# Mamba scan: the input delta·u·B and the convolution moved to TensorE

## The chip, the cores and the metric

The kernel runs on one core of a Trainium2 chip. The metric is the device time of one execution in microseconds (us). Three runs of the kernel before gave 3393.25, 3393.28 and 3399.04 us, so its time is 3393.28 us, the median. A profile is one more execution, recorded instruction by instruction; its own span counts from the first to the last instruction.

Engines: PE is TensorE (PEld its loading of weights), DVE is VectorE, ACT is ScalarE, POOL is GpSimd, SP is the engine that only issues DMAs here. Each works its own queue in order.

## The reference, cut to what matters

Two layers run one after the other; the change is in the first one, a Mamba block beside a feed-forward network with fp4-quantized weights and activations. There are 8 batches of 512 tokens, 256 features, 512 inner channels and 16 states.

```python
xz = jnp.einsum('bld,ed->ble', x, W_in)
x_in, z = (xz[..., :d_inner], xz[..., d_inner:])
xc = lax.conv_general_dilated(x_in.transpose(0, 2, 1), conv_w, (1,), [(k - 1, 0)], feature_group_count=d_inner)
u = jax.nn.silu(xc + conv_b[None, :, None]).transpose(0, 2, 1)
x_dbl = jnp.einsum('bld,ed->ble', u, W_xproj)          # delta_raw, B_ssm, C_ssm
delta = jax.nn.softplus(jnp.einsum('blr,dr->bld', delta_raw, W_dt) + b_dt)
A = -jnp.exp(A_log)

def step(h, inp):
    d_t, u_t, B_t, C_t = inp
    dA = jnp.exp(d_t[:, :, None] * A[None])
    h = dA * h + (d_t * u_t)[:, :, None] * B_t[:, None, :]
    y_t = jnp.einsum('bdn,bn->bd', h, C_t)
    return (h, y_t)
...
y = (ys.transpose(1, 0, 2) + D_param * u) * jax.nn.silu(z)
return jnp.einsum('bld,ed->ble', y, W_out)
```

Before this the input is normalized, and its output and that of the feed-forward network are added to it.

## The kernel before

**Layout.** Channels lie on the 128 partitions (four chunks of channels, NC = 4) and time runs along the free dimension, so that one VectorE instruction scans 512 tokens of one state for 128 channels. A step g of the main loop handles two states of one chunk of one batch: 8 batches x 4 chunks x 8 pairs of states = 256 steps (STEPS = 32 a batch).

**A step.** `decay` (ACT) makes exp(delta·A) for two states into `da`. `spread_b` (PE) copies a row of B over all partitions: a bf16 matmul of a selector `sel` with `bp`, three bf16 pieces of B that together carry fp32 precision, into a PSUM tile `bu`. `product` (DVE) multiplies `bu` in place by delta·u (`du`). `scan` (DVE) runs the recurrence from `da` and `bu` into `hh`. `times_c` (POOL) multiplies `hh` by C, which a DMA on SP's queue has spread over the partitions (`cb`, fetched two steps ahead). `sum_states` (PE) turns `hh` and adds up the 16 states in the PSUM tile `y`.

**The order.** All engines keep the program order that is written out here (the class `Ordered`). At step g the loop issues: the C fetch of g+2, the sums of g-2 (or g-3), the decays of g+1, the first scan of g, the spreads of g+1, one piece of every active strand, the product with C of g-1, the second scan of g, and the products of g+1. A strand is a generator; between two of its `yield`s lie the instructions of one step. A `yield` gives how many PSUM banks of the pool `pmm` (MM = 4) the next piece needs and keeps, and the strand waits for a later step if they aren't free. Where the next chunk isn't in `ready`, the loop runs strands alone, without scans (line 769).

**The strands.** `head(b+1)` loads and normalizes x (`xn`, `xt`), projects it (`ps_in`), convolves with four taps (one on ACT, three on DVE over `cv`), makes `u`, the projection `ps_xp`, the pieces of B, and from `ps_dt` the softplus delta and `du` for two chunks at a time. It is started five steps before batch b begins. `ffn(b)` quantizes and multiplies; `output(b)` projects the gated result with `w_o`; `z` and `finish` make the gate and close a chunk; `fp4_weights` and `rotary_tables` prepare weights during batches 0 and 1.

**PSUM.** Eight banks: four for strands, three for `bu` (one state each), one for `y`.

Line numbers of the scan stage's instructions in the profile are all L50, the helper that keeps the order; the tiles' names tell them apart. The second layer (lines 800 to 1369) isn't edited.

Of the kernel before, what the change touches and what calls it, by code (L numbers as in the profile page):

```python
# [17 lines left out]
P = 128  # L18
# [18 lines left out]
RD, RC, PIECES = 32, 48, (0, 64, 96)  # L37
# [18 lines left out]
def tile_kernel(ctx: ExitStack, tc: tile.TileContext, a: dict, out: bass.AP):  # L56
# [57 lines left out]
    with ExitStack() as s0:  # L114
# [6 lines left out]
        MM = 4  # L121
        pmm = s0.enter_context(tc.tile_pool(name="pmm0", bufs=MM, space=PSUM))
        pbu = s0.enter_context(tc.tile_pool(name="pbu0", bufs=3, space=PSUM))
# [5 lines left out]
        def load_x(b):  # L129
            t = w1.tile([P, NT, D], FP, tag="x", bufs=3, name=f"x_{b}")  # L130
            sp.dma_start(t, a["x"][b].rearrange("(t p) d -> p t d", p=P))
            return t

        x_first = load_x(0)
        w_in = load(w0, chunks(a["w_in"]), [P, KC, 2 * DI], "w_in")
# [3 lines left out]
        w_xp = load(w0, chunks(a["w_xp"]), [P, NC, P], "w_xp")  # L139
# [5 lines left out]
        w_o = load(w0, chunks(a["w_o"]), [P, NC, D], "w_o")  # L145


        sel = w0.tile([P, NS, P], BF, name="sel")
        every = w0.tile([P, NS], BF, name="every")

        def constants():
            act.activation(a_neg, a_neg, AF.Exp)
            dve.tensor_scalar(a_neg, a_neg, -1.0, None, ALU.mult)
            dve.tensor_copy(every, ident[:, :NS])
            for at in PIECES[1:]:
                dve.tensor_tensor(every, every, ident[:, at : at + NS], ALU.add)
            for n in range(NS):
                dve.tensor_copy(sel[:, n, :], every[:, n : n + 1].to_broadcast([P, P]))
# [169 lines left out]
        def rotary_tables():  # L328

            for l in range(DEPTH):  # L330
                tab = rot.tile([P, 2, L], FP, tag="e", bufs=2, name="tab")
                tab = tab.rearrange("p i (t d) -> p (i t) d", d=LD).rearrange("p (i t) d -> p i t d", t=NT)
                sp.dma_start(tab, a["rotary"])
                qss = []
                for name in ("q_scale", "k_scale"):
                    qss.append(sm.tile([P, LD], FP, tag="qs", bufs=2, name="qs"))
                    sp.dma_start(qss[-1], a[name][l].unsqueeze(0).to_broadcast([P, LD]))
                yield 0, 0
                yield 0, 0
                dve.tensor_scalar(qss[0], qss[0], 8.0, None, ALU.mult)  # L340
                hd = LD // 2
                lo, hi = slice(0, hd), slice(hd, LD)
                for i, qs in ((0, qss[0]), (2, qss[1])):
                    for at, cols, sc in ((i, lo, lo), (i, hi, hi), (i + 1, lo, hi), (i + 1, hi, lo)):
                        by = qs[:, sc].unsqueeze(1).to_broadcast([P, NT, hd])
                        dve.tensor_tensor(tab[:, at, :, cols], tab[:, at, :, cols], by, ALU.mult)
                        if cols is hi:
                            yield 0, 0
                sp.dma_start(tab_d[l], tab)
                yield 0, 0  # L350

        made, xs, u_, z_, ready, through = {}, {}, {}, {}, set(), set()

        def head(b):

            x = xs[b] = load_x(b) if b else x_first
# [12 lines left out]
            dve.reciprocal(rs, rs)  # L369
            xn = w1.tile([P, NT, D], FP, tag="xn", name="xn")  # L370
# [8 lines left out]
            xt = w1.tile([P, KC, L], FP, tag="xt", name="xt")  # L379
# [8 lines left out]
            def put(k, ps):  # L388
                act.copy(xt[:, k, :], ps)
# [7 lines left out]
            def project(c, _):  # L397
                ps = pmm.tile([P, L], FP, tag="mm", name="ps_in")
                for k in range(KC):
                    pe.matmul(  # L400
                        ps, w_in[:, k, c * P : (c + 1) * P], xt[:, k, :], start=(k == 0), stop=(k == KC - 1)
# [8 lines left out]
            def tap0(c, ps):  # L410
                cv = rot.tile([P, L], FP, tag="cv", bufs=2, name="cv")
# [20 lines left out]
            stages = [(project, 0, 1), tap0, taps12, (tap3, 1, 0), silu]  # L432
            for i, need in enumerate(skewed(range(NC), stages, 2)):
                while i + 1 == len(stages) and b - 2 in u_:
                    yield 0, 0
                yield need
            u = u_[b]
            yield 1, 1
            ps = pmm.tile([P, L], FP, tag="mm", name="ps_xp")
            for c in range(NC):  # L440
                pe.matmul(ps, w_xp[:, c, :], u[:, c, :], start=(c == 0), stop=(c == NC - 1))
            yield 0, -1
            xd = w1.tile([P, L], FP, tag="xd", bufs=1, name="xd")
            act.copy(xd, ps)
            c_d = dram.tile([NS, L], FP, tag="c_d", name="c_d")
            sp.dma_start(c_d, xd[RC : RC + NS, :])

            bp = w1.tile([P, L], BF, tag="bp", name="bp")
            act.copy(bp, ps)
            yield 0, 0  # L450

            def pieces():
                for at in PIECES[1:]:
                    pool.tensor_tensor(xd[at:, :], xd[at:, :], bp[at:, :], ALU.subtract)
                    yield 0, 0
                    act.copy(bp[at:, :], xd[at:, :])
                    yield 0, 0

            delta = w1.tile([P, NC, L], FP, tag="delta", name="delta")
            du = w1.tile([P, NC, L], FP, tag="du", name="du")
            made[b] = xn, xt, bp, c_d, delta, du
# [6 lines left out]
            def parts(c, ps):  # L470
                act.activation(delta[:, c, :], ps, AF.Relu, bias=b_dt[:, c : c + 1])
                act.activation(ps, ps, AF.Abs, bias=b_dt[:, c : c + 1])
                act.activation(ps, ps, AF.Exp, scale=-1.0)
                act.activation(du[:, c, :], ps, AF.Copy, bias=1.0)
                return ps

            def rests(c, e, ps):
                w = du[:, c, :]
                dve.scalar_tensor_tensor(e[:, c % 2, :], w, 1.0, ps, ALU.subtract, ALU.subtract)

            def second(c0, ps):
                return ps, rank(c0 + 1)

            def third(c0, st):
                e = rot.tile([P, 2, L], FP, tag="e", bufs=2, name="e")
                rests(c0, e, st[0])
                return e, parts(c0 + 1, st[1])

            def fifth(c0, st):
                rests(c0 + 1, *st)  # L490
                return st[0]

            def logs(c0, e):
                w = du[:, c0 : c0 + 2, :]
                act.activation(w, w, AF.Ln)
                return e

            def sums(i):
                def f(c0, e):
                    w = du[:, c0 + i, :]  # L500
                    by.tensor_tensor(w, w, e[:, i, :], ALU.subtract)
                    return e
                return f

            def deltas(i):
                def f(c0, e):
                    c = c0 + i
                    by.tensor_tensor(delta[:, c, :], delta[:, c, :], du[:, c, :], ALU.add)
                    by.tensor_tensor(du[:, c, :], delta[:, c, :], u[:, c, :], ALU.mult)
                    ready.add((b, c))  # L510
                    return e
                return f

            by = pool if b else dve
            rest = pieces()
            stages = [
                (lambda c0, _: rank(c0), 0, 1), parts, (second, 0, 1), (third, 1, 0), lambda _, st: st, (fifth, 1, 0),
                logs, sums(0), sums(1), deltas(0), deltas(1),
# [958 lines left out]
```

## Time and profile before

| what | value |
|---|---|
| median of three runs | 3393.28 us |
| span of the profiled execution | 3396.9 us |
| first scan starts | 45.4 us |
| last scan starts | 1374.5 us |
| second layer's first PE instructions | about 1405 us |
| busy over the span: PE, DVE, ACT, POOL | 88%, 71%, 52%, 47% |
| POOL product with C (`hh`<-`hh`,`cb`), 256 of them | 604.4 us, 2363 ns each |
| ACT decay (`da`), 512 of them | 355.2 us, 718 ns each |
| ACT table loads, 242 of them | 310.5 us, 1283 ns each |
| `y` turns on PE, 2048 of them | 300.9 us busy |

How to read it: a share of busy time over the whole span mixes two stages. The scan stage is the first 1390 us or so. In the groups of the profile a line reads: source line, engine, operation, output tile <- input tiles, shapes, number, then busy us and mean ns of one, then idle time of the engine before them and who ended it. A busy PE is not a PE at its peak: matmuls overlap, and their ends are modelled. PEclk is the clock that TensorE was granted, as a share of full speed. fp32 matmuls appear as two instructions, turns (`is_transpose`) as one.

### The profile page before, as it was taken

To read this page: it belongs to the slowest core of one execution; us is meant where nothing else is said; L and a number is where in the kernel's file an instruction comes from. 1 tells how busy PE (TensorE), PEld (TensorE's weight loads), DVE (VectorE), ACT (ScalarE), POOL (GpSimd) and SP (SyncE) were. 2 spreads that over 40 slices of the span, in tenths; PEclk is the share of its full clock that TensorE was granted. 3 is DMA by queue.
4 is the path that set the end of the run, shared out by engine and by line. 5 is a ranking of instruction groups with operands and counts; after the bars stand their busy time and mean duration, and the time that the engine had idled before them with its cause. 6 is when DMAs were issued, how large, how long until landed. Compare 5 with 4: busy or idle time off the path is not lost.

```text
span 3396.9 us, 43346 instructions
## 1 busy us (share of the span) xinstructions
PE 2974.0 (88%) x15235; PEld 1723.3 (51%) x15236; DVE 2422.4 (71%) x4792; ACT 1771.3 (52%) x3500; POOL 1581.5 (47%) x1141
## 2 busy tenths in 40 slices
PE   5667787877777877899999999999999999999998
PEld 2434454545454555555554555555545545545545
DVE  7979898999999999665566466466556557556544
ACT  5666777676767776244254245244334334433533
POOL 3876777787868687333133133123223223312412
PEclk7768898989898889899999999999999999999999
DMA  3322233323232333301111101111110100100100
GB/s 107 120 90 104 97 109 102 125 93 125 96 125 96 119 105 137 108 32 52 40 38 52 45 32 52 46 49 38 42 58 32 64 33 32 64 33 32 58 33 7
DMA packets 88865, 239.55 MB, mean 71 GB/s; under 512 B 9656, under 2 KB 42424, under 8 KB 88648
## 3 DMA queue, kind: packets, MB, share of 16 engines
q1 hardware_dynamic: 87496, 232.59, 19.9%
q10 hardware_dynamic: 1152, 4.19, 0.3%
q8 instruction: 121, 1.98, 0.2%
q14 instruction: 96, 0.79, 0.1%
HBM read 227.05 MB, written 9.70 MB: 70 GB/s over the span
## 4 chain that ended last, share of the span: by engine, by line
PE 59%; DVE 26%; ACT 6%; issue 4%; POOL 4%; DMA 1%; DVEq 0%; SPq 0%; POOLq 0%; ACTq 0%
PE ps_qkv L1131 10%; DVE hh L50 10%; PE ps_g L1310 5%; PE ps_a L1310 4%; PE ps_wo L1274 3%; PE lo L1244 3%; DVE bu L50 3%; PE ps_y L1345 3%; PE ps_w L1328 3%; PE pt L1230 2%; PE y L50 2%; PE ps_ls L1183 2%; PE ps_gu L50 2%; PE ps_d L50 2%; DVE nm L997 2%
## 5 line engine op out<-in xcount | busy, mean ns | idle before, releaser
L50 POOL TENSOR_TENSOR hh<-hh,cb 128x1024 f32<-128x1024 f32 x256 | 604.4, 2363 | 177.5 <-DVE hh L50 109.4
L50 DVE TENSOR_TENSOR_SCAN hh<-da,bu 128x512 f32<-128x512 f32 x512 | 613.7, 1207 | 0.2 <-ACT da L50 0.2
L50 ACT ACTIVATE da<-delta,a_neg 128x512 f32<-128x512 f32 x512 | 355.2, 718 | 290.1 <-DVE hh L50 285.8
L50 PE MATMUL bu<-bp,sel 128*128 128x512 bf16 x511 | 197.3, 423 | 231.3 <-DVE hh L50 230.2
L50 PE MATMUL y<-ident,hh 128*128 128x128 f32 x2048 | 300.9, 298 | 89.9 <-POOL hh L50 89.7
L50 PEld LDWEIGHTS y<-ident,hh 128*128 128x128 f32 x2048 | 264.7, 155 | 179.7 <-POOL hh L50 131.8
L50 DVE TENSOR_TENSOR bu<-du,bu 128x512 f32<-128x512 f32 x512 | 324.9, 681 | 37.1 <-PE bu L50 36.8
L50 ACT ACT_TABLE_LOAD x242 | 310.5, 1283 | 23.9 <-DVE x L50 11.1
L1221 POOL TENSOR_TENSOR pr<-pr,lrs 128x512 f32<-128x512 f32 (+1 forms) x256 | 234.6, 933 | 176.6 <-DVE lrs L1219 137.7
L1150 POOL TENSOR_TENSOR r<-r,r 128x512 f32<-128x512 f32 x128 | 162.8, 1272 | 286.5 <-DVE r L1148 240.8
L1202 ACT ACTIVATE pr<-ps_ls,nm 128x256 f32<-128x256 f32 (+1 forms) x512 | 221.6, 448 | 122.4 <-DVE nm L1196 119.3
L1146 DVE TENSOR_TENSOR r<-ps_qkv,tab 128x512 f32<-128x512 f32 x128 | 88.2, 689 | 199.3 <-ACT sq L1145 195.4
L1316 ACT ACTIVATE gl<-ps_g,b 128x512 f32<-128x512 f32 x96 | 65.9, 687 | 304.1 <-PE ps_g L1310 304.1
L1048 ACT ACTIVATE pt_e<-ps_st 128x512 f32<-128x512 f32 x320 | 166.7, 596 | 107.0 <-PE ps_st L1042 100.8
L886 POOL MEMSET sa<- 128x1 f32 x16 | 1.6, 98 | 450.2 <-DVE sf L1332 356.9
L1091 POOL TENSOR_TENSOR x1s<-x1s,bsum 128x256 f32<-128x256 f32 x32 | 23.2, 724 | 370.3 <-DVE x1s L1090 370.3
L1196 DVE CUSTOM_DVE_ANT_0 ps_ls<-ps_ls,mask 128x256 f32<-128x256 f32 (+1 forms) x512 | 184.3, 422 | 5.7 <-PE ps_ls L1183 4.7
L1310 PE MATMUL ps_g<-hn,wf 128*128 128x512 f32 x384 | 183.0, 599 | 4.0 <-DVE hn L1299 2.6
L1131 PE MATMUL ps_qkv<-wqkv,sf 128*128 128x512 f32 x384 | 182.4, 608 | 0.0
L1131 PE MATMUL ps_qkv<-wqkv,s 128*128 128x512 f32 x384 | 179.8, 604 | 0.2 <-DVE r L1148 0.2
L1317 DVE SCALAR_TENSOR_TENSOR ht<-ps_a,b,gl 128x512 f32<-128x512 f32 x80 | 60.0, 750 | 157.5 <-PE ps_a L1310 157.5
L1230 PE MATMUL pt<-ident,pr 128*128 128x128 f32 x896 | 130.9, 281 | 33.0 <-POOL pr L1221 28.3
(216 smaller groups left out, 6314.5 us busy)
## 6 DMA issues: line engine op xcount, KB each, us to landing
cb<-c_d SPq DMA_DIRECT2D x256, 512.0 KB, 3.6
wqkv<-in_wqkv SPq DMA_DIRECT2D x16, 1536.0 KB, 6.8
wf<-in_wf SPq DMA_DIRECT2D x16, 1408.0 KB, 11.2
wf<-in_wf SPq DMA_DIRECT2D x16, 768.0 KB, 4.7
tab<-tab SPq DMA_DIRECT2D x18, 512.0 KB, 3.6
wo<-in_wo SPq DMA_DIRECT2D x16, 512.0 KB, 3.9
x<-in_x SPq DMA_DIRECT2D x8, 512.0 KB, 5.0
x<-x ACTq DMA_DIRECT2D x8, 512.0 KB
```

Source lines behind the costliest of these rows:

```text
L50: return self.tc.keep_in_program_order(getattr(self.engine, name)(*args, **kwargs))
L1048: act.activation(pt, banks[g], AF.Exp)
L1131: pe.matmul(ps, shifted(s, k, t * P, P), wqkv[:, k, i * IN : (i + 1) * IN], start=(k == 0), stop=(k == KC - 1),)
L1150: pool.tensor_tensor(r1[:, i], r1[:, i], r2, ALU.add)
L1196: last = dve.tensor_tensor_reduce(at, at, msk[:, 2 * P - nk :], -1.0, 3e38, ALU.add, ALU.min, nm[:, i : i + 1])
L1202: act.activation(pr[:, at], banks[r][:, at], AF.Exp, bias=nm[:, i : i + 1], scale=-1.0, accum_out=rs[:, i : i + 1],)
L1221: pool.tensor_tensor(ph, ph, rs.unsqueeze(2).to_broadcast([P, 2, nk]), ALU.mult)
L1230: pe.transpose(pt[:, j * P : (j + 1) * P], pr[:, j * P : (j + 1) * P], ident)
L1244: pe.matmul(o[r * LD : (r + 1) * LD, i * P : (i + 1) * P], lv[:, keys[j], h * LD : (h + 1) * LD], prts[r][:, (i * nkt + j) * P : (i * nkt ...
L1274: pe.matmul(ps, wo[:, c, m * P : (m + 1) * P], ot[:, c, :], start=(c == 0), stop=(c == IN // P - 1),)
L1310: pe.matmul(dst, wf1[:, k, off : off + P], hn[:, k, :], start=(k == 0), stop=(k == KC - 1))
L1328: pe.matmul(ps, wf2[:n, c, m * P : (m + 1) * P], ht[c][:n], start=(c == 0), stop=(c == NHC - 1),)
```

## The change

The spreads and products are replaced. For each chunk, delta·u is turned on TensorE (`halves_turned`, eight matmuls with the identity, one for each 64 tokens) and copied back by ACT, so that 64 tokens of the first half of time lie on partitions 0 to 63 and 64 tokens of the second half on 64 to 127. For each batch VectorE makes eight tiles `bd`, one for each pair of states: diagonals of B, 64 x 64 for each block of tokens, the two states interleaved. `inputs` then multiplies, eight fp32 matmuls of 64 rows by 128 columns a step, the two halves of time into two different PSUM banks; `scan` reads every second word. The pieces of B in bf16, `sel` and `every` go.

From batch 1 on the convolution is eight fp32 matmuls a chunk on TensorE (two halves of the features times four taps, from `xt` with four leading zeros and weights `w_c`, scaled by the taps on POOL), with bias and silu in one ACT instruction. Batch 0 keeps its taps.

To make room, PSUM's strand banks fall from four to three and `bu` has two tiles of two banks; `delta` and `du` become five buffers of one chunk each, shared by batches (HELD); the softplus runs chunk by chunk; x is loaded a second time, late, for the sums; `w_o` is loaded for every batch; `head(b+1)` starts 16 steps before batch b begins; several strands wait for buffers of others.

```diff
-RD, RC, PIECES = 32, 48, (0, 64, 96)
+RD, RC, XR = 32, 48, 64
+HELD = 5
+XP = 4
+HL = P // 2
...
-        MM = 4
+        MM = 3
         pmm = s0.enter_context(tc.tile_pool(name="pmm0", bufs=MM, space=PSUM))
-        pbu = s0.enter_context(tc.tile_pool(name="pbu0", bufs=3, space=PSUM))
+        pbu = s0.enter_context(tc.tile_pool(name="pbu0", bufs=2, space=PSUM))
...
-            dve.tensor_copy(every, ident[:, :NS])
-            for at in PIECES[1:]:
-                dve.tensor_tensor(every, every, ident[:, at : at + NS], ALU.add)
-            for n in range(NS):
-                dve.tensor_copy(sel[:, n, :], every[:, n : n + 1].to_broadcast([P, P]))
+            dve.tensor_tensor(twice, ident[:, :HL], ident[:, HL:], ALU.add)
+            for k in range(KC):
+                for i in range(4):
+                    pool.tensor_tensor(w_c[:, k, i, :], w_x[:, k, :], taps[i // 2][:, i % 2, :], ALU.mult)
...
+        def halves_turned(ps, x, n):
+
+            for t in range(NT):
+                for r in range(2):
+                    pe.matmul(
+                        ps[r * HL : (r + 1) * HL, t * n : (t + 1) * n],
+                        x[:, (r * NT + t) * HL : (r * NT + t + 1) * HL], ident[:n, :n], start=True, stop=True,
+                    )
...
-            stages = [(project, 0, 1), tap0, taps12, (tap3, 1, 0), silu]
-            for i, need in enumerate(skewed(range(NC), stages, 2)):
-                while i + 1 == len(stages) and b - 2 in u_:
-                    yield 0, 0
-                yield need
+            def convolve(k):
+                def f(c, ps):
+                    if k == 0:
+                        ps = pmm.tile([P, L], FP, tag="mm", name="ps_in")
+                    for i in range(4):
+                        pe.matmul(
+                            ps, w_c[:, k, i, c * P : (c + 1) * P], xt[:, k, XP - 3 + i : XP - 3 + i + L],
+                            start=(k == i == 0), stop=(k == KC - 1 and i == 3),
+                        )
+                    return ps
+                return f
+
+            def biased(c, ps):
+                if c == 0:
+                    u_[b] = w1.tile([P, NC, L], FP, tag="u", name="u")
+                act.activation(u_[b][:, c, :], ps, AF.Silu, bias=conv_b[:, c : c + 1])
+
+            while b - 2 in u_:
+                yield 0, 0
+            if b:
+                yield from skewed(range(NC), [(convolve(0), 0, 1), convolve(1), (biased, 1, 0)], 2)
+            else:
+                yield from skewed(range(NC), [(project, 0, 1), tap0, taps12, (tap3, 1, 0), silu], 2)
...
+            def diagonals():
+                yield 1, 1
+                ps = pmm.tile([P, L], FP, tag="mm", name="ps_bt")
+                halves_turned(ps, xd[:NS, :], NS)
+                yield 0, -1
+                bt = sm.tile([P, NT, NS], FP, tag="bt", bufs=2, name="bt")
+                act.copy(bt, ps[:, : NT * NS].rearrange("p (t n) -> p t n", n=NS))
+                yield 0, 0
+                for i in range(NS // 2):
+                    while b and clock[0] < b * STEPS - NS // 2 + i:
+                        yield 0, 0
+                    bd = rot.tile([P, NT, HL, 2], FP, tag="bd", bufs=NS // 2 + 1, name="bd")
+                    dve.tensor_tensor(
+                        bd, twice.unsqueeze(1).unsqueeze(3).to_broadcast([P, NT, HL, 2]),
+                        bt[:, :, 2 * i : 2 * i + 2].unsqueeze(2).to_broadcast([P, NT, HL, 2]), ALU.mult,
+                    )
+                    diags.append(bd)
                     yield 0, 0
...
+            def turned(c, _):
+                ps = pmm.tile([P, L], FP, tag="mm", name="ps_du")
+                halves_turned(ps, du[b, c], P)
+                return ps
+
+            def put_du(c, ps):
+                act.copy(du[b, c], ps)
+                ready.add((b, c))
...
             stages = [
-                (lambda c0, _: rank(c0), 0, 1), parts, (second, 0, 1), (third, 1, 0), lambda _, st: st, (fifth, 1, 0),
-                logs, sums(0), sums(1), deltas(0), deltas(1),
+                (lambda c, _: rank(c), 0, 1), parts, (rests, 1, 0), logs, sums, deltas, (turned, 0, 1), (put_du, 1, 0),
             ]
-            for need in skewed(range(0, NC, 2), stages, 2 if b else len(stages) - 4):
-                next(rest, None)
-                yield need
+            for c in range(NC):
+                k = b * NC + c - HELD
+                while b and (b - 1, NC - 1) not in ready or k >= 0 and divmod(k, NC) not in gated:
+                    yield 0, 0
+                active[skewed([c], stages, 1)] = 0, 0
+                for _ in range(3):
+                    yield 0, 0
...
-        def spread_b(g, i):
+        def inputs(g):
+
             b, c, n = at(g)
-            bu = pbu.tile([P, L], FP, tag="bu", name="bu")
-            pe.matmul(bu, sel[:, n + i, :], made[b][2], start=True, stop=True)
-            spreads.setdefault(g, []).append(bu)
-
-        def product(g):
-            b, c, n = at(g)
-
-
-            for bu in spreads[g]:
-                dve.tensor_tensor(bu, made[b][5][:, c, :], bu, ALU.mult)
-            hs[g] = rot.tile([P, 2, L], FP, tag="h", bufs=4, name="hh")
+            bu = spreads[g] = pbu.tile([P, 2, NT, 2 * HL], FP, tag="bu", name="bu")
+            for t in range(NT):
+                for r in range(2):
+                    rows = slice(r * HL, (r + 1) * HL)
+                    pe.matmul(
+                        bu[:, r, t, :], du[b, c][rows, t * P : (t + 1) * P],
+                        diags_[b][n // 2][rows, t, :, :].rearrange("p n i -> p (n i)"), start=True, stop=True,
+                    )
 
         def scan(g, i):
-            dve.tensor_tensor_scan(hs[g][:, i, :], decays[g][i], spreads[g][i], 0.0, ALU.mult, ALU.add)
+            if i == 0:
+                hs[g] = rot.tile([P, 2, L], FP, tag="h", bufs=4, name="hh")
+
+            bu = spreads[g].rearrange("p r t n -> p (r t n)")[:, i::2]
+            dve.tensor_tensor_scan(hs[g][:, i, :], decays[g][i], bu, 0.0, ALU.mult, ALU.add)
...
-                start(g - 5 if b else 0, (head, b + 1))
+                start(g - 16 if b else 0, (head, b + 1))
...
-            while g + 2 < total and at(g + 2)[:2] not in ready:
+            while g + 2 < total and not able(g + 2):
                 step()
```

Not shown: the loads of `taps`, `w_x` and `w_z` in place of `w_in`; the second load of x in `ffn` and the load of `w_o` in `output`; the rotary tables made in two halves; `able(g)`, which asks that the chunk is in `ready` and that the diagonal of the pair exists.

## The prediction

> **What bounds the kernel now.** I first read the slices of the page, to see which stage the edit touches.
>
> ```profile
> PE   5667787877777877899999999999999999999998
> DVE  7979898999999999665566466466556557556544
> POOL 3876777787868687333133133123223223312412
> PEclk7768898989898889899999999999999999999999
> ```
>
> The scan stage is the first sixteen slices of 85 us. There VectorE is at nine tenths, TensorE at seven to eight at a granted clock of 0.8 to 0.9. After it TensorE is full at full clock, and nothing is edited. Then I cut the stage by batch. The copies of a batch's last sum (delta<-y) start at 595.2, 759.2 and 923.1 us, so a steady batch takes 163.9 us; the busy times between them:
>
> ```profile
> 174.60:243.40 68.80, 39.29 (x139) 24.16 (x140) 44.27 (x65) 43.24 (x63) 53.97 (x37) 0.64 0.20 70
> 759.20:923.10 163.90, 126.36 (x570) 83.38 (x568) 152.49 (x199) 119.27 (x164) 126.88 (x75) 0.90 0.32 110
> 923.10:1087.00 163.90, 126.31 (x569) 83.31 (x568) 152.52 (x199) 119.30 (x165) 126.92 (x75) 0.90 0.32 110
> 1246.10:1381.20 135.10, 108.05 (x540) 77.57 (x538) 132.12 (x169) 81.39 (x114) 105.74 (x57) 0.92 0.36 127
> ```
>
> Columns: stretch, length, then busy us of PE, PEld, DVE, ACT, POOL, clock, DMA share, GB/s. VectorE is the bound (152.5 of 163.9, 93%), but PE, POOL and ACT stand at 126, 127 and 119. The first row is the end of batch 0, which stalls (DVE 44 of 69). The waits of 100 to 1430 us agree on who leads:
>
> ```profile
> PE bu L50 <- DVE hh L50: 203.2, 154, 3.9
> PE y L50 <- POOL hh L50: 83.0, 46, 11.6
> ```
>
> TensorE waits for scans (for a free `bu`) and for POOL's product with C.
>
> **VectorE, removed and added.** Per batch there are 32 steps of two states.
>
> ```profile
> L50 DVE TENSOR_TENSOR_SCAN hh<-da,bu 128x512 f32<-128x512 f32 x512 | 613.7, 1207 | 0.2 <-ACT da L50 0.2
> L50 DVE TENSOR_TENSOR bu<-du,bu 128x512 f32<-128x512 f32 x512 | 324.9, 681 | 37.1 <-PE bu L50 36.8
> ```
>
> The product goes: 324.9/8 = 40.6 us a batch. The convolution's three taps go from batch 1 on: 12 of 728 to 748 ns, 8.8 us. The diagonals come: eight multiplies 128x512 with two SBUF inputs. No row has that operand shape; the nearest is the add delta<-delta,du of batch 0, 0.69 us where POOL is idle (42.35 us) and 1.25 us in the mean of four. I take 1.0, so 8 us (5.5 to 10). VectorE: 152.5 - 40.6 - 8.8 + 8 = 111 us. The scan now reads every second word of PSUM, which no row shows. Its bounds: 1.165 us as now (two in 2.33), or at most 1.27: the product reads PSUM at 0.635 us per 512 words, so 1024 words would need that. I take 1.165; the other adds 6.7 us to an engine that is no longer the bound.
>
> The Trainium skill ("SBUF — State Buffer", Who interferes with whom) says that a VectorE instruction with two SBUF inputs is kept out by a GpSimd instruction that reads SBUF. By it a diagonal could wait out a whole 2.36 us product on POOL: 8 x 3 = 24 us, VectorE 127, still not the bound. The mean of four above is what the trace shows of it.
>
> **TensorE, from rows at full clock.** "Busy" here holds tails and slow clock, so I count start to next start in dense stretches.
>
> ```profile
> 632.42 1.88 PE L50 MATMUL ps_in<-xt,w_in 128*128 128x512 f32 x4
> 634.14 1.89 PE L50 MATMUL ps_o<-w_o,u 128*128 128x256 f32 x8
> 635.86 1.04 PE L50 MATMUL y<-ident,hh 128*128 128x128 f32 x8
> 636.74 0.38 PE L50 MATMUL bu<-bp,sel 128*128 128x512 bf16 x1
> ```
>
> An fp32 matmul is two instructions. Four of 512 columns take 1.72 us (0.43 each), eight of 256 take 1.72, eight turns of `y` 0.88 (0.87 elsewhere). The later stage has the new shapes:
>
> ```profile
> 1838.47 1.04 PE L1122 MATMUL pt_qk<-ident,r 128*128 128x128 f32 x8
> 1839.44 1.16 PE L1183 MATMUL ps_ls<-lkt,lqt 64*128 64x128 f32 x16
> 1840.53 1.09 PE L77 MATMUL ps_tr<-ident,xn 128*128 128x128 f32 x8
> 1848.61 0.66 PE L1244 MATMUL lo<-prt,lv 128*64 128x128 f32 x8
> 1849.20 1.13 PE L1183 MATMUL ps_ls<-lkt,lqt 64*128 64x256 f32 x8
> ```
>
> Sixteen instructions of 64 rows by 128, two row halves into two banks, which is exactly `inputs`, take 1.09 us. Without overlap it would be 16 x 0.108 = 1.73 (half of the 256-column row); I take 1.09, the identical shape. Eight turns before them take 0.97 and not 0.87, so entering the half-row form costs 0.10.
>
> - Out: two bf16 spreads, 0.43 x 32 = 13.8 us.
> - In: `inputs`, (1.09 + 0.10) x 32 = 38.1 us (to 58.6 without overlap).
> - In: the convolution, 16 instructions of 0.43 a chunk for 4: +12 x 0.43 x 4 = 20.6 us.
> - In: `turned`, 16 of 64 columns a chunk; 8 take 0.59 (above), so 1.18 x 4 = 4.7 us. B's own turn, 16 tiny ones, about 1 us.
>
> Net +50.6 us. The present batch in the same spacing is: y 27.8, bu 13.8, gate and up 16 groups of four at 1.24 (19.8), ps_d 4 x 2.88 (11.5), ps_in, ps_z, ps_o 6.9 each, ps_xp and ps_dt 3.4 each, the turns ps_i, ps_y, ps_tr 6.0: 106.4. Its busy time of 126.4 at clock 0.90 is 106.4/0.90 x 1.07. After: 157 us dense, x 1.07 = 168 us of busy time even at full clock. TensorE thus becomes the bound, at more than the batch takes now.
>
> The rule that speaks against the change is in the Trainium skill ("TensorEngine Tiling (Array Packing)", Key Properties): a change of tiling mode drains the engine. It has no figure; the trace's is the 0.10 above on entry. Leaving is inside the 1.09, so rule and sum differ by nothing I can price.
>
> **ACT, POOL, DMA.** ACT loses cv (4 x 0.78) and three casts (1.8), gains four copies of the turned du (2.3), one of B, and twice as many Ln calls, each between two table loads of 1.28: up to +5.1. Result about 122 us. POOL loses two corrections, 2.3 us: 124.5. Both are hidden under TensorE at 4 us a step, but unevenly: in some 13 steps fall 13 products with C (30.6 us), four chunks of sums and deltas at 3.84, xn's 5.3 and about 11 of quantization, 62 us or 4.8 a step, so `y` still waits for POOL there. On SP's queue come, per batch, a second load of x and one of w_o, 512 KB each. Each can wait for its single buffer, and the cb loads queue behind it; these are fetched two steps (10 us) ahead against landings of 3.6 to 5 us, so I cost it at nothing, and at some 5 us a batch if that lead is gone. Three PSUM banks for strands in place of four: counting the strands' yields, the first chunk of the next batch is ready one step before it is needed, so no gap, but without reserve.
>
> **New waits.** `inputs` waits, as the spread did, for the scan that frees `bu`, now two pairs in place of three single tiles; behind it in TensorE's queue stand the strands' matmuls and the next `y`, and for those wait ACT's silu and copies, and POOL through `hh`. As TensorE sets the pace the scan two steps back is long done, so I price it at nothing; if VectorE led again it would be the 203 us above, idle time of an engine that doesn't lead.
>
> **Sum.** Ten steps with the convolution hold 6.0 us of PE work each (27.5 of it, 5.0 of gate and up, 3.4 ps_xp, 1.7 ps_z, ten times 2.1 for y and inputs), the other 22 hold 4.4, nearly what POOL needs there. PE in the later stage is busy 97% of the time; here it also loses some POOL waits (10.6 us a batch now, perhaps half of that left). 168/0.97 = 173 us a steady batch, +9 for each of batches 2 to 6: +46. Batch 7 has no head: VectorE falls from 132 to 92 and PE is about 122, for 135 now: -12. Batch 0 has no convolution of its own on TensorE and loses 32 steps of VectorE products, but the matrices of weights times taps (eight POOL multiplies of 1.27, 10 us) come into it: -8. Batch 1 (181 us now) stays. +46 - 12 - 8 = +26 us. Against this execution's span of 3396.9 that is 3423. The three runs have a median of 3393.28, with 3399.04 at the top, so the span stands 3.6 above the median; I forecast **3420 us**.
>
> **Rivals.**
> - *Faster: TensorE packs tightly.* For it: all new work is long, ready early and needs one wait a step, and the clock would rise to 1.00. If batches 2 to 6 run near the dense count, 158 us, they give 5 x -6 = -30, batches 0, 1 and 7 -20, -15 and -15: -80, so 3313. It decides from a steady batch under 168 us (5 x 4 pays for the 20 gained elsewhere). Against it: PE waits for POOL 83 us already.
> - *Much slower: one more rotation stall.* The three strand banks or the single x, xqt buffers make a strand late; scans then stop for whole steps, as at 200 to 216 us now. 185 us a batch: +105, and nothing gained in the others: 3500. For it: the reserve of one step. Against: the counted order fits.
> - *The relief doesn't come:* the scan slows on the gapped read. It decides from 2.0 us a scan (111 + 64 x 0.84 = 165); at twice the time, 186/0.93 = 200 a batch, some 3680. Against it: the 1.27 bound above.
>
> **Numbers.** Chances: forecast (steady batch 168 to 180) 0.50, tight TensorE 0.34, rotation stall 0.13, slow scan 0.03. The forecast's own range is 3385 to 3455. To leave no more than 0.2 out, the range reaches to the faster case and to the stall: 3315 to 3515; it takes the 5 us of the SP queue but not inputs without overlap (+20 a batch). A measurement tells 0.2%, 7 us, from no change. About 0.07 lies within it, most from the forecast: faster 0.35, same 0.07, slower 0.58.
>
> **What would show it.** Right: PE at nine tenths and clock near 1.0 in the scan slices, VectorE at six to seven; sixteen `bu` instructions in about 1.1 us; steady batches of 168 to 178; few waits of PE for `hh` of DVE. Wrong: scans over 1.3 us; `bu` groups of 1.7; PE under 155 a batch; gaps in all engines at a batch's border; DMA as a releaser of cb.

## The result and the profile after

| | before | changed |
|---|---|---|
| median (runs) | 3396.16 us (4) | 3503.58 us (4) |
| lowest to highest | 3393.25 to 3399.18 | 3497.44 to 3509.36 |
| span of the profiled execution | 3396.9 | 3496.6 |

The changed kernel takes 1.0317 times as long, 95% interval 1.0298 to 1.0335: some 107 us, where 24 to 27 were forecast. It is slower, as forecast, and inside the range given, but four times as much slower as the sum said.

The slices of the changed kernel's page, busy tenths of 40 equal stretches of 87 us:

```profile
PE   5879999998989898999999999999999999999998
DVE  6687656666676658755655655665566466556544
POOL 3796766767585848722322241132133123222312
PEclk7989999999999999989999999999999999999999
```

The scan stage is now the first seventeen slices. There TensorE has gone from seven or eight tenths to eight or nine, VectorE from nine to between five and eight, the clock from eight or nine tenths to nine. The bound has changed engine, as forecast. Cut at the copies of each batch's last sum (columns as in the prediction; the rows are batch 1, batch 4 and batch 7):

```profile
234.91:432.39 197.48, 186.14 (x1212) 126.92 (x1212) 139.68 (x169) 138.60 (x193) 141.55 (x86) 0.96 0.34 114
802.57:985.25 182.68, 167.56 (x1151) 116.40 (x1150) 117.46 (x131) 118.97 (x168) 127.25 (x73) 0.95 0.31 104
1345.49:1477.15 131.66, 125.04 (x976) 97.07 (x976) 105.09 (x111) 83.38 (x120) 110.28 (x60) 0.96 0.38 129
```

TensorE's work in a steady batch is 167.56 us; 168 was forecast. But the batch takes 182.7 us and not 173. The waits between 100 and 1500 us have turned round:

```profile
DVE hh L53 <- PE bu L53: 222.7, 101, 6.6
PE y L53 <- POOL hh L53: 57.5, 31, 5.2
PE bu L53 <- DVE hh L53: 24.5, 18, 3.3
```

Now the scans wait for their input (222.7 us), and TensorE waits for a scan only 24.5 us (203.2 before). Its wait for GpSimd ahead of `y` has fallen from 83.0 to 57.5 us. Where in batch 4 TensorE's idle time lies, the same table shows for four stretches of it, the third being that of the convolution:

```profile
802.57:823.00 20.43, 14.08 (x131) 10.95 (x129) 15.91 (x22) 16.80 (x26) 19.06 (x14) 0.93 0.23 78
823.00:854.00 31.00, 30.91 (x246) 25.45 (x246) 19.21 (x20) 14.14 (x22) 26.59 (x17) 0.94 0.42 137
854.00:923.00 69.00, 69.00 (x380) 41.68 (x376) 31.97 (x40) 40.84 (x52) 28.52 (x15) 1.00 0.27 92
923.00:985.25 62.25, 53.57 (x401) 38.33 (x401) 50.37 (x51) 47.20 (x68) 53.08 (x31) 0.92 0.33 110
```

For 100 us (the second and third stretch) TensorE isn't idle at all; in the convolution's 69 us VectorE and POOL are busy for less than half. In the other 83 us TensorE is idle for 15 and its granted clock is 0.92 to 0.93. The single groups of matmuls take what was forecast (start, duration, count):

```profile
881.44 1.04 PE L53 MATMUL y<-ident,hh 128*128 128x128 f32 x8
882.41 1.16 PE L53 MATMUL bu<-bd,du 64*128 64x128 f32 x16
883.50 3.70 PE L53 MATMUL ps_in<-xt,w_c 128*128 128x512 f32 x8
887.04 1.35 PE L53 MATMUL ps_gu<-w_u,xqt 128*128 128x352 f32 x4
```

From start to next start: 0.97 us for `y` before `inputs`, 1.09 for `inputs`, 3.54 for half a chunk of convolution (eight instructions; 3.43 where they are quickest). The scan on every second word, and the other two new groups of the stage (busy, mean ns, idle before):

```profile
L53 DVE TENSOR_TENSOR_SCAN hh<-da,bu 128x512 f32<-128x512 f32 x512 | 602.1, 1203 | 274.8 <-PE bu L53 227.2
L53 PE MATMUL bu<-bd,du 64*128 64x128 f32 x4096 | 320.9, 300 | 34.0 <-DVE hh L53 33.9
L53 PE MATMUL ps_in<-xt,w_c 128*128 128x512 f32 x448 | 206.9, 604 | 0.0
```

The scan takes 1203 ns (1207 before).

### The profile page after: what moved, and what is told of

It reads as the page before. It is cut to its first block, busy times and chain, and to the rows that moved or that the text cites. A ratio compares the mean times of both kernels' runs of the same rounds, so it can differ in the third digit from the quotient of the medians.

```text
span 3496.6 us, 52045 instructions
## 1 busy us (share of the span) xinstructions
PE 3280.7 (94%) x19796; PEld 1976.5 (57%) x19796; DVE 2186.0 (63%) x4242; ACT 1783.8 (51%) x3527; POOL 1593.4 (46%) x1141
## 4 chain that ended last, share of the span: by engine, by line
PE 73%; DVE 11%; POOL 8%; ACT 6%; issue 2%; DMA 1%; POOLq 0%; SPq 0%; DVEq 0%; ACTq 0%
PE ps_qkv L1181 10%; PE bu L53 5%; PE ps_in L53 5%; PE ps_g L1360 5%; PE y L53 4%; PE ps_a L1360 4%; POOL hh L53 3%; PE ps_wo L1324 3%; PE ps_gu L53 3%; PE lo L1294 3%; PE ps_y L1395 3%; PE ps_w L1378 2%; PE pt L1280 2%; DVE hh L53 2%; PE ps_d L53 2%
## 5 line engine op out<-in xcount | busy, mean ns | idle before, releaser
L53 DVE TENSOR_TENSOR_SCAN hh<-da,bu 128x512 f32<-128x512 f32 x512 | 602.1, 1203 | 274.8 <-PE bu L53 227.2
L53 PE MATMUL bu<-bd,du 64*128 64x128 f32 x4096 | 320.9, 300 | 34.0 <-DVE hh L53 33.9
L53 PE MATMUL y<-ident,hh 128*128 128x128 f32 x2048 | 282.1, 286 | 65.3 <-POOL hh L53 59.2
L53 PEld LDWEIGHTS bu<-bd,du 64*128 64x128 f32 x4096 | 270.3, 201 | 90.7 <-issue 75.2
L53 PEld LDWEIGHTS y<-ident,hh 128*128 128x128 f32 x2048 | 244.5, 147 | 131.6 <-POOL hh L53 79.4
L53 PE MATMUL ps_in<-xt,w_c 128*128 128x512 f32 x448 | 206.9, 604 | 0.0
```

Source lines behind the costliest of these rows:

```text
L53: return self.tc.keep_in_program_order(getattr(self.engine, name)(*args, **kwargs))
```

## The experiments

All times are medians, all ratios are to the kernel before, run on the same chip at the same time (3397 to 3399 us). Three questions were put, one after the other. The letters A, B and C of the first four expectations are those texts' own; from e7 on they are defined anew, in the texts themselves.

### Is it TensorE's work?

**e1_conv_dve**: the changed kernel with the convolution of batches 1 to 7 back on ScalarE and VectorE too. The line that decides it (`w_c` and its making go as well, and `cv` gets two buffers of its own):

```diff
- yield from skewed(range(NC), [(convolve(0), 0, 1), convolve(1), (biased, 1, 0)], 2)
+ yield from skewed(range(NC), [(project, 0, 1), (all_taps, 1, 0), silu], 2)
```

> The convolution of batches 1 to 7 goes back to ScalarE and VectorE (one project matmul pair, four taps in one step, as many steps as now); inputs stay on TensorE. TensorE loses 12 x 0.43 x 4 = 20.6 us a batch, VectorE gets 9 back. Theory A (two phases: TensorE is full only in the ten convolution steps, in the others POOL, ACT and PE share the bound): the convolution phase shrinks by 15 to 20, a steady batch takes 162 to 167 in place of 182, in all 3380 to 3410. Rival B (TensorE alone sets all of a batch at a constant 0.92 busy): 147/0.92 = 160, 3350 to 3370. Rival C (late strands and three banks): no gain, 3490 to 3510.

**e3_inputs_bf16**: the convolution stays on TensorE; the turned delta·u and the diagonals of B are rounded to bf16, so that `inputs` is eight instructions a step in place of sixteen. The turned delta·u also gets buffers of its own (`dub`).

```diff
- bd = rot.tile([P, NT, HL, 2], FP, tag="bd", ...)
+ bd = rot.tile([P, NT, HL, 2], BF, tag="bd", ...)
+ du[b, c] = w1.tile([P, L], BF, tag="dub", bufs=HELD, name="dub")   # in put_du
```

> The turned delta*u and the diagonals are kept in bf16, so the scan's input is rounded to bf16 factors and its matmuls are eight one-pass instructions a step in place of sixteen two-pass ones: 1.19 us become 0.5 to 0.6, 19 to 21 us a batch less on TensorE, spread evenly over all steps. Theory A: only the steps in which TensorE is full profit, some 17 of 32: 10 to 12 us a batch, 3410 to 3430. Rival B: all of it, 21/0.92 = 23 a batch, 3320 to 3345. Rival C: none, 3490 to 3510.

**e2_deltas_dve**: sums and deltas of all batches on VectorE, so that POOL reaches the products with C sooner (`by = dve`).

> Sums and deltas of the softplus (three 128x512 operations a chunk) go from POOL to VectorE in every batch; nothing else. POOL loses 4 x 3.84 = 15.4 us a batch, VectorE gets 8 to 15; both lie outside the convolution steps. Theory A: the other steps shrink by 6 to 10 us a batch, 3430 to 3460. Rival B (TensorE alone): at most the 8.7 us that TensorE waits for POOL in a batch, and most of that comes back as other waits: 3480 to 3505. Rival C: none, 3495 to 3510.

**e5_conv_deltas**: e1 and e2 together.

> Both edits of the first two runs together: convolution on VectorE, sums and deltas on VectorE, inputs on TensorE. Loads of a batch: TensorE 147, VectorE 135, POOL 112, ACT 122. Theory A: both phases shrink, 152 to 158 a batch, 3310 to 3350, faster than the kernel before the change. Rival B: like the first run alone, 3350 to 3370. Rival C: 3490 to 3510.

| | us | ratio, 95% interval | batches 2 to 6, mean | batch 4 | of it PE, DVE, ACT, POOL |
|---|---|---|---|---|---|
| changed | 3503.58 | 1.0317 [1.0298, 1.0335] | 182.6 | 182.7 | 168, 117, 119, 127 |
| e1 | 3420.89 | 1.0073 [1.0058, 1.0088] | 171.0 | 166.2 | 147, 129, 124, 129 |
| e3 | 3422.15 | 1.0072 [1.0056, 1.0089] | 171.6 | 169.2 | 150, 117, 118, 128 |
| e2 | 3501.74 | 1.0310 [1.0295, 1.0326] | 182.8 | 184.6 | 170, 135, 119, 112 |
| e5 | 3427.53 | 1.0093 [1.0077, 1.0108] | 171.3 | 164.2 | 147, 138, 124, 112 |

Batch 4 is one batch, and it is a short one in e1, e3 and e5; the means, cut in the same way, are the safer measure (164.3 in the kernel before). Taking 21 or 17 us of work a batch off TensorE, by two different edits, gives 83 and 81 us of the 107 lost (58 and 55 of them in batches 2 to 6). Taking 15 us off POOL gives nothing, while VectorE gets 17: in e2, between 600 and 1250 us, `y` waits for POOL 12.7 us in place of 34.4, and the time stays. So TensorE's added work is the cause of three quarters of the loss, and POOL's work isn't. But neither e1 nor e5 falls below the kernel before, though VectorE has 129 us of work in e1 where it had 152. Of the numbers on record, theory A's held for e3 alone (it missed e1 by 11 us, e2 by 42 and e5 by 78), and the lowest ones of e1, e3 and e5 (3310 to 3370) all failed: with 147 us of TensorE's work something else sets the batch.

### What holds the batch at 164 to 171 us?

Before, e1 and e5 stand at 164 to 166 us in batch 4, with VectorE at 152, 129 and 138, and at 164.3, 171.0 and 171.3 over batches 2 to 6. Four kernels, all with the convolution on VectorE as in e1. **e7_conv_bf16** has the bf16 inputs of e3 too.

> Convolution of batches 1 to 7 back on ScalarE and VectorE (as e1_conv_dve) and the turned delta*u and the diagonals rounded to bf16, so that inputs is one-pass (as e3_inputs_bf16). PE then has about 147 - 17 = 130 us of work a batch, VectorE 129, ScalarE 124, POOL 129. Theory A (TensorE's work alone sets the batch, which was 166 us at 147 of PE, 169 at 150, 183 at 168: work over 0.89 to 0.92): 145 a steady batch, five to six batches 20 us shorter than in e1_conv_dve, 3290 to 3320. Theory E (a floor of about 164 us a batch that the strands and the hand-over from engine to engine set, whichever engine is relieved; before, e1 and e5 all stand at 164 to 166): 3395 to 3425. Theory B (strands that come late at a batch's border add a fixed share): about 3350, batches of 150 to 155 with the gaps left.

**e8_third_u** has a third buffer for `u`, so that the convolution needn't wait for it.

```diff
- u_[b] = w1.tile([P, NC, L], FP, tag="u", name="u")
+ u_[b] = w1.tile([P, NC, L], FP, tag="u", bufs=3, name="u")
- while b - 2 in u_:
+ while b - 3 in u_:
```

> e1_conv_dve with a third buffer for u, so that the convolution of batch b+1 no longer waits for the output product of batch b-1 and starts at step 0 to 6 of the batch before in place of 9 to 12. Steps that only strands make, with no scan in them, fall from 13 to 3 in the program's order (3 in place of 5 for batches 1 and 2, none after). No engine's work changes. Theory B (late strands at the border hold the batch): 4 to 6 us a step taken away, 3360 to 3385. Theory A (TensorE's work sets it): 3410 to 3425, no change. Theory E (a floor of hand-overs): 3400 to 3420.

**e9_bf16_third_u** has the edits of both e7 and e8.

> e7_conv_bf16 and e8_third_u together: one-pass inputs, convolution on VectorE, third u buffer. If A and B are both right, 3250 to 3290 and a steady batch of 140 to 148; if only A, as e7_conv_bf16 (3290 to 3320); if only B, as e8_third_u (3360 to 3385); if E, 3390 to 3420.

**e10_da_ring** has six buffers of `da` in place of four, and fp32 inputs.

```diff
- da = rot.tile([P, L], FP, tag="da", bufs=4, name="da")
+ da = rot.tile([P, L], FP, tag="da", bufs=6, name="da")
```

> e1_conv_dve with six da buffers in place of four, so that ScalarE's exp of step g+1 waits for the scans of step g-2 and no longer for those of g-1 (25 us of ScalarE's idle time a batch end with a scan). Theory D (ScalarE held up by the scans is late with the strands' copies and with da): 3370 to 3400, waits of da for hh under 8 us a batch. Theories A, B and E: 3412 to 3428, no change.

Measured: e7 3395.03 (ratio 0.9999 [0.9984, 1.0013]), e8 3432.48 (1.0104 [1.0087, 1.0121]), e9 3409.12 (1.0042 [1.0027, 1.0057]), e10 3394.95 (0.9992 [0.9980, 1.0003]). Starting the convolution some six to ten steps earlier gains nothing in e8 and loses 12 us (e8 lies 12 us above the numbers of theory E, e9 within them), so the late strands, the mechanism of the rival with a rotation stall, are out as what holds e1. That they don't hold the changed kernel either is read from its own trace: in its batches 3 to 6 no two successive scans start more than 6.8 us apart. Batches 1 and 2 have one longer distance each, of 17.3 and 11.1 us. That rival had the right number for a steady batch (185 us, measured 182.7) and nearly for the whole (3500) for the wrong reason.

e7 gains 26 us in place of 100 to 130, and e10 gains the same 26 with no engine's instructions changed. The windows of a batch of e1, of e7 and of e10, one row from each:

```profile
768.54:934.72 166.18, 146.81 (x1093) 106.30 (x1094) 129.31 (x144) 124.17 (x171) 128.58 (x74) 0.97 0.34 115
```

```profile
756.20:921.48 165.28, 134.97 (x826) 90.43 (x824) 126.89 (x144) 124.00 (x171) 128.93 (x74) 0.87 0.35 116
```

```profile
750.45:911.24 160.79, 144.20 (x1089) 105.07 (x1090) 129.14 (x144) 123.23 (x172) 129.02 (x74) 0.98 0.36 119
```

In e7 no engine is busy for more than 82% of this batch, and the batch is nearly as long as in e1; over batches 2 to 6 the means are 171.0 in e1, 166.4 in e7 and 166.8 in e10. The wait that e10's edit was made for goes (us, times, longest, between 600 and 1250 us), first e1, then e10:

```profile
ACT da L53 <- DVE hh L53: 97.3, 50, 5.5
```

```profile
ACT da L53 <- DVE hh L53: 6.6, 5, 4.7
```

With four buffers, used in turn (a ring), the exp of step g+1 must wait for the scans of step g-1, and behind it in ScalarE's queue stand the strands' copies. An engine at 75% of its time held the others up by where it had to wait.

### Which hand-overs, and does the same hold with the convolution on TensorE?

A hand-over is a place where one engine waits for what another has made or frees.

**e12_bf16_da** is e7 with six `da` buffers.

> e7_conv_bf16 (convolution on VectorE, one-pass inputs: TensorE at 132 us of work a batch) with six da buffers. Theory A+D (the ring of da hid what TensorE's relief was worth): the ring gives more than the 26 us it gave e10_da_ring, 3320 to 3355, batches of 150. Theory F (TensorE's queue is held by y, which waits for POOL's product with C, and behind it stand inputs and all strands; neither change touches that): 3375 to 3392, batches of 158 to 163. Additive without either: 3365 to 3372.

**e13_inputs_da** is e3 with six.

> e3_inputs_bf16 (convolution on TensorE, one-pass inputs, 3422) with six da buffers. Theory D (ScalarE held up by the scans is late with everything behind da, whichever engine leads): as much as in e10_da_ring, 3390 to 3402. Theory A (with the convolution on TensorE its work sets the batch and a lead of ScalarE is worth nothing): 3415 to 3428.

**e14_late_y** is e12 with the sum over states a step later and a fifth `hh` buffer, so that TensorE seldom meets a product that POOL has yet to make; **e15_late_y_fp32** is the same on e10.

```diff
- for k in (g - 3, g - 2):
-     if 0 <= k < total and (k % (NS // 2) == 0) == (k == g - 3):
+ for k in (g - 4, g - 3):
+     if 0 <= k < total and (k % (NS // 2) == 0) == (k == g - 4):
- for k, f in ((-4, z), (1, finish)):
+ for k, f in ((-4, z), (2, finish)):
- hs[g] = rot.tile([P, 2, L], FP, tag="h", bufs=4, name="hh")
+ hs[g] = rot.tile([P, 2, L], FP, tag="h", bufs=5, name="hh")
```

> e12_bf16_da with the sum over states (y) one step later in TensorE's order and a fifth hh buffer for it. Theory F (y waiting for POOL's product, 49 us in four batches of e7_conv_bf16, holds inputs and the strands behind it): 10 to 15 us a batch less than e12_bf16_da, 3300 to 3340, waits of y for hh of POOL under 3 us a batch. Theory E (a floor of other hand-overs): within 10 us of e12_bf16_da.

> e10_da_ring (convolution on VectorE, inputs in fp32: TensorE at 144 to 147 us a batch, 3395) with the sum over states one step later and a fifth hh buffer. Theory F: 3340 to 3365, batches of 153 to 156, clearly under the kernel before. Theory E: 3385 to 3402. Theory A (TensorE at 0.9 is as full as it gets): 3385 to 3402 too, with the wait of y for hh gone and that of scans for bu as long as now (59 us in four batches).

**e16_bf16_late_y** is e3 with the late sum and five `hh` buffers; **e17_after_late_y** is the changed kernel with the late sum and, for want of room, four.

> e3_inputs_bf16 (convolution on TensorE, one-pass inputs, 150 us of TensorE's work a batch in 169) with the sum over states one step later and a fifth hh buffer. Theory F (TensorE's idle share, 19 us a batch there, is its wait for POOL's product with C ahead of y, 50 us in four batches): 8 to 12 us a batch less, 3350 to 3375. Theory A with the uneven load (TensorE full in the convolution's third of the batch and idle elsewhere, whatever y waits for): 3405 to 3425.

> The changed kernel itself with the sum over states one step later, and still four hh buffers (there is no room for a fifth), so that a scan may wait for the y of four steps before. Theory F: TensorE's idle 15 us a batch shrinks by the 9 us that y waits for POOL, 3440 to 3465, waits of y for hh under 15 us in the whole stage. Theory A with the uneven load: 3485 to 3510. Slower than 3515 if the ring of four now holds the scans, with scans waiting for y in the table of waits.

| | convolution on | edit | us | ratio, 95% interval | gain by the edit | batches 2 to 6, mean, without and with it |
|---|---|---|---|---|---|---|
| e12 | VectorE | e7 + ring | 3363.36 | 0.9896 [0.9881, 0.9910] | 32 | 166.4, 161.1 |
| e14 | VectorE | e12 + late y | 3326.44 | 0.9787 [0.9771, 0.9804] | 37 | 161.1, 160.7 |
| e15 | VectorE | e10 + late y | 3378.46 | 0.9948 [0.9932, 0.9963] | 16 | 166.8, 165.1 |
| e13 | TensorE | e3 + ring | 3422.89 | 1.0074 [1.0059, 1.0089] | -1 | 171.6, 171.1 |
| e16 | TensorE | e3 + late y | 3411.93 | 1.0041 [1.0029, 1.0052] | 10 | 171.6, 171.9 |
| e17 | TensorE | changed + late y | 3488.20 | 1.0261 [1.0245, 1.0278] | 15 | 182.6, 180.9 |

With the convolution on VectorE the hand-overs decide: the ring gives 26 to 32 us, most of it in batches 2 to 6. The later sum gives 16 where TensorE still has 144 us of work and 37 where it has 128, but hardly in these batches: of the 37 us, 13 lie between the first and the last scan of batch 7 and 10 in batch 1. So e14 met the time forecast by theory F (3300 to 3340) but not its 10 to 15 us a batch. The wait itself is mostly gone; in e14 and in e12, between 600 and 1250 us:

```profile
PE y L53 <- POOL hh L53: 9.1, 7, 3.8
```

```profile
PE y L53 <- POOL hh L53: 62.0, 31, 7.9
```

With it on TensorE the same edits give -1 and 10 to 15 us. Part of e17's gain went into a new wait: with four buffers the scans wait 72.3 us for `y` in the whole stage, which e16's fifth buffer avoids. Another part went into a load: TensorE waits for `w_o`, which the changed kernel fetches for every batch, 18.2 us in e17 and 21.4 in e16, where it waited 1.2 us in the changed kernel and 4.3 in e3 (19.1 and 19.5 in e14 and e15, after 12.9 and 12.3 in e12 and e10). So the gains of 10 and 15 us need not be all that the later sum is worth there; no run has it without that wait. The numbers of theory F failed for e16 and e17 by over 20 us, and for e15 by 13; those of the uneven load held for e16 and e17, and e12 came 2 us below its additive range.

The batch of e17 that holds 809 to 988 us, cut as above (the middle row is the convolution's stretch):

```profile
809.37:853.00 43.63, 38.48 (x305) 30.81 (x302) 35.26 (x37) 24.54 (x39) 40.14 (x25) 0.96 0.37 119
853.00:923.00 70.00, 70.00 (x394) 43.13 (x394) 32.10 (x41) 45.25 (x57) 32.75 (x19) 1.00 0.31 98
923.00:988.43 65.43, 61.08 (x450) 43.82 (x448) 54.70 (x56) 54.04 (x77) 54.01 (x32) 0.87 0.32 107
```

The full stretch is as long as before (70 us), the idle time beside it has gone from 15 to 9.5 us. That what is left comes from the uneven load, a convolution packed into some ten of 32 steps, agrees with this, but wasn't tried: to spread it, it has to start earlier, which takes a third `u` (8 KB a partition, where there wasn't room for a fifth `hh` of 4).

e14 beats both kernels: 2.1% under the kernel before, 5% under the changed one. It keeps the change's inputs, rounded to bf16, and leaves the convolution where it was. e15, with fp32 inputs, is 0.5% under the kernel before. Whether the same two edits help the kernel before by themselves wasn't tried, so that e14 is faster than the kernel before doesn't show that moving the inputs is worth anything.

## Why the prediction was right and wrong

| term | forecast | measured |
|---|---|---|
| TensorE's work, steady batch | 168 | 167.6 |
| batches 2 to 6 together | +46 | +92 (16.7, 19.0, 18.8, 16.3, 21.0) |
| batch 1 | 0 | +16 |
| batch 7 | -12 | -3.5 |
| batch 0 | -8 | -8.5 |
| the span | +26 | +99.7 (3.8 of it outside the batches) |

**Right**: which engine becomes the bound; the prices of `inputs`, of the convolution and of entering the half-row form (1.09, 0.43 to 0.44 an instruction, 0.10 us); the net work on TensorE; the scan's speed on every second word; next to no loss by DMA (TensorE waits 1.2 us for it between 100 and 1480 us); batch 0. That 167.6 us met 168 is in part luck: the sum was 157 us of dense work and 7% for tails, at full clock, while batch 4's busy time holds some 6 us of matmuls at half clock (worked out in the last section), so that about 161 are left at full speed.

**The step that failed is "168/0.97 = 173 us a steady batch".** The mechanism holds, the size of one term was off: the share of time that TensorE is busy. 0.97 was read from the later stage, where nothing but TensorE's work counts. In this stage it is 167.6/182.7 = 0.92 (batches 1 to 7: 1155 us of work in 1242, 0.93). The 9.5 us that this makes a batch are 47 us over five batches, all of the +46 that was missing there. The prediction had noted that the ten steps with the convolution hold 6.0 us of TensorE's work and the others 4.4, the latter nearly what POOL needs; it then used one share for the whole batch. What the runs showed in its place is a full stretch, for which the batch pays in full, beside stretches in which the hand-overs between four engines keep TensorE at 82% (67.7 us of 82.7). Of the 15 us idle, `y` waiting for POOL is 8.7, in five waits; "perhaps half of that left" had been the forecast (5 of 10.6). The rest are seven waits of 0.5 to 2.4 us for VectorE and ScalarE. Taking the wait for POOL away (2.2 us left in e17 between 600 and 1250 us, of 34.4) shortened e17's whole run by 15 us, not by the 47 missing; as other waits came in its place, what it costs by itself stays open.

**"Batch 1 (181 us now) stays"** was a slip. TensorE had 138.9 us of work in it and has 47 us more now, 186.1 (batch 4 got 41); at that it can't stay at 181. This is the other large part of what was missing, 16 us. **Batch 7**: TensorE's work came to 125.0 us where 122 were forecast, and it too needs 0.95 of the batch: 131.7 and not 123.

**Diagonals**: 1.0 us each was forecast, 8 us a batch; measured were 1.32 us in the mean of all 64, 10.6 a batch, and 12.6 in batch 4. Of the eight of batch 4 the first three are shown:

```profile
940.63 0.63 DVE L53 TENSOR_TENSOR bd<-twice,bt 128x512 f32<-128x512 f32 x1
944.01 2.02 DVE L53 TENSOR_TENSOR bd<-twice,bt 128x512 f32<-128x512 f32 x1
949.26 0.68 DVE L53 TENSOR_TENSOR bd<-twice,bt 128x512 f32<-128x512 f32 x1
```

The same instruction takes 0.63 to 2.44 us in this batch. The eleven of the 64 during which POOL had no instruction running took 0.67 to 0.69 us; all that took over 0.7 ran beside one. The Trainium skill ("SBUF — State Buffer", Who interferes with whom) has a rule that fits: a VectorE instruction with two SBUF inputs contends with a GpSimd instruction that reads SBUF. By whole products the prediction made 24 us of them; the trace has half of that in batch 4. VectorE, at 117 us a batch, had room for it.

**The rivals.** Tight TensorE needed a batch under 168 us; with the convolution and two-pass inputs both on TensorE no run came near it. The slow scan didn't occur. What no rival held is the second limit that showed when TensorE was relieved: some 161 to 171 us a batch in the mean of batches 2 to 6. e10 and e12 moved it by 4 to 5 us a batch without changing any engine's instructions, so part of it is where ScalarE's queue waits; what sets the rest isn't shown.

## What to carry to other kernels

When work moves to an engine that thereby leads, its new batch time is its work over the busy share that this stage can reach with this order, and that share isn't to be borrowed from another stage: steps in which the engine is full are paid in full, and idle time elsewhere doesn't make up for them. Relieving the leading engine is worth little if a second limit stands just beside it; here VectorE lost 23 us of work a batch (e1) for no gain, until a ring of buffers was lengthened (a gain in every steady batch) and one product was consumed a step later (in e14 a gain mostly in batches 1 and 7). Before trading engines in a kernel whose engines all stand at 75 to 93%, these two edits are worth a try: they cost 4 KB a partition each and no work. A gain should be read over all steady batches: batch 4 alone showed none from e1 to e7, where the mean fell by 4.6 us.

## What the hardware showed that was not expected

TensorE ran at half speed for some microseconds after it had stood idle. After 5.17 us of waiting for POOL, in the changed kernel:

```profile
823.09 1.97 PE L53 MATMUL y<-ident,hh 128*128 128x128 f32 x8 [5.17 <-POOL hh L53]
824.99 2.08 PE L53 MATMUL bu<-bd,du 64*128 64x128 f32 x16
827.00 1.98 PE L53 MATMUL ps_z<-xt,w_z 128*128 128x512 f32 x4
```

`y` and `inputs` take twice as long as at 881 us, the projection behind them the usual time; the granted clock from 820.20 to 827.03 us is 0.50. It doesn't take one long wait: after waits of 0.57, 1.25 and 1.44 us between 923 and 934 us the clock is 0.50 from 932.84 to 939.67 us, and the groups in it take twice as long too. A third such stretch follows a wait of 2.35 us (0.50 from 970.39 to 973.80). Against their usual durations the groups in these three took 1.9, 2.8 and 1.6 us longer, so an estimate is 6 us of batch 4 beside its 15 idle ones: a wait of TensorE can cost more than itself. Over whole batches the busy share alone doesn't give the clock: in batch 4 it was 0.87 in e7 (TensorE busy 82%), 0.97 in e1 (88%) and 0.92 in e3 (89%). The 125 to 138 us that TensorE was busy in e7's batches 2 to 6 hold some of it.

In bf16 the inputs took 0.33 us from start to next start, in place of 1.09. e3, eight matmuls between `y` and the convolution:

```profile
850.55 0.40 PE L53 MATMUL bu<-bd,dub 64*128 64x128 bf16 x8
850.88 3.70 PE L53 MATMUL ps_in<-xt,w_c 128*128 128x512 f32 x8
```

That is 24 us a batch (32 x 0.76) at full speed; TensorE's busy time fell by 17, at a granted clock of 0.92 for the batch in place of 0.95.
